# Three attention layers as one sequence of steps, with one list of stages placed between them

## The chip, the cores and the metric

The kernel runs on one core of a Trainium2 chip. The metric is device time in microseconds. The kernel before took 1880.95 us, the median of three runs (1877.2 to 1883.09). Matmuls run on TensorE (PE in the profile), elementwise work on VectorE (DVE), ScalarE (ACT) and GpSimd (POOL), and transfers are issued mostly by SyncE (SP), the indirect ones by POOL.

## The reference

The state x has 4 batches of 512 tokens with 128 features. Four layers follow each other, each of the form: normalize x, run a mixer s and a mixture of experts g on the normalized rows, and add s times silu(g):

```python
xn = _layernorm(x, axis=-1)
s = _L1_attn_ref(xn, ...)           # layer 0: selective scan; 1: causal; 2: rope; 3: distance bias
g = _silu(_L1_ffn_ref(xn, ...))     # experts
x = x + s * g
```

Each attention has 16 heads of 8 features. Layer 1 is causal, and its result is added to xn and normalized again. Layer 2 divides exp(q k) with rope by the sum of exp(q k) without rope, and is normalized again too. Layer 3 subtracts a distance times a slope of the head. The experts are: layer 1, top 2 of 4, with silu(x w1) * (x w3); layer 2, top 2 of 8; layer 3, top 1 of 16, each expert taking at most 160 tokens, those with the highest gate value.

## The kernel before

**Attention.** Work goes by groups: a batch and 4 heads, 16 groups in all. A group takes four steps, one for each block of 128 rows, so an attention has 64 steps, counted k = 0 to 63. In a step, `first_pass` (two heads at a time) makes scores, of which VectorE takes the maximum in layers 1 and 3 (L926) or, in layer 2, the sum of exponentials (L921, L922). `probabilities` makes the scores again transposed and takes the exponential on ScalarE (L956, two per step); in layer 1 POOL clears what lies above the diagonal (`affine_select`, L960). One step later `apply` multiplies with the values (L972). In layers 1 and 3 the first pass runs 8 and 7 steps ahead of the probabilities, so those attentions begin at step -8 and -7; groups are spread (L909) a further four steps ahead.

**Preparing a batch.** `project` (L868 and on) makes q, k and the values of a batch, splits q and k into bf16 parts on ScalarE, VectorE and POOL (L849 to L859, for layer 2 with rope before, L883 to L889), and `spread` moves the parts into the operand blocks by 8 transfers of SP a group (16 in layer 2). After a group `finish` transposes and divides, and after a batch's last group it applies the output matrix.

**Between the instructions of a step** there are two places (`slot`). A place takes jobs due (projects, finishes, the second half of `shift`), then one stage of the list `Work`, and if that was empty, one piece of the generator `beside`, the experts' work of the layer. A piece that ends with "free" uses no engine of the attention, one with "dve" may be followed only in the first place of a step.

**The layers.** Layer 1: its routing (gates, ranks, 32 scatters of rows into expert order, L1232) is `beside` its attention. Its experts (`Routed.run`, L1288 for the first matmuls, L1268 for the second) run behind the attention, 19 tiles of 256 rows. `back` fetches the results of a batch with 8 indirect gathers (L1308), weighs them (L1317, L1318), and `turn` does silu (by exponential and reciprocal, L1333 to L1338), the product and sum (L1340, L1341), the next layer's norm (`rows_norm`, L366 to L382) and the transposes (L1346) of that batch. Batch 0 is turned before attention 2 begins, batches 1 to 3 in its places. Layer 2's experts (`moe2`) are `beside` attention 2. Behind attention 2, `post_norm` (L1104, L1105), `end_layer` (L394 to L400) and `begin_layer` (L319, L326) handle all 16 blocks at once, then attention 3 starts. Layer 3's gate, ranking (L1477 to L1489, 32 pieces), 16 scatters, 16 experts in 18 overlapped rounds (L1555 to L1578) and 16 gathers (L1598) are `moe3`, `beside` attention 3; what is left when the attention ends runs behind it, and `end_layer` closes.

**Order.** Inside `tc.manual_schedule` the listed engines run in the order in which the code is written. For attentions 1 and 2 these are PE, ACT and DVE; SP and POOL are left to the scheduler. For layer 1's experts and attention 3 all five are listed. Each engine runs its queue in order.

Of the kernel before, what the change touches and what calls it, by code (L numbers as in the profile page):

```python
# [2 lines left out]

# [16 lines left out]
P = 128  # L20
# [207 lines left out]
def kernel(ctx: ExitStack, tc: tile.TileContext, ap: dict):  # L228
# [108 lines left out]
    class Work:  # L337


        def __init__(self):  # L340
            self.queue = []

        def add(self, key, stages):
            self.queue.append((key, stages))

        def step(self):

            while self.queue:
                got = next(self.queue[0][1], None)
                if got is not None:  # L350
                    return got
                self.queue.pop(0)

        def need(self, key):

            while any(k == key for k, _ in self.queue):
                self.step()

    work = Work()
# [32 lines left out]
    def end_layer(i, s, y):  # L392
# [3 lines left out]
        out = ap["out"].rearrange("(c p) d -> p c d", p=P) if i == 3 else None  # L396
        for h in range(2):
# [3 lines left out]
            if i == 3:  # L401
                nc.sync.dma_start(out=out[:, cs, :], in_=x[:, cs, :])
# [44 lines left out]
    def weighted_bias(acc, cw, b2, e):  # L447

        for q in range(NC // 4):
# [3 lines left out]
            cwT = small.tile([e, 512], F32, tag="cwT", name="cwT", bufs=1)  # L453
# [68 lines left out]
    def layer0(ctx0, mp, fp, s_out, acc):  # L522
# [182 lines left out]
        with tc.manual_schedule(engines=engines | {mybir.EngineType.SP}):  # L705
# [32 lines left out]
            for n in range(last):  # L738
                now = n
                b, r = divmod(n, 32)  # L740
                if n == 0:
                    in_stages(0, 1)
                    after(2, weighted_bias, acc, cw, b2, E0)
# [40 lines left out]
    def attention(i, lp, xnT, pads, vaug, s_io, beside=iter(()), done=lambda b: None):  # L784
# [9 lines left out]
        wqk = lp.tile([P, 2, P], F32, name="wqk")  # L794
        nc.sync.dma_start(out=wqk, in_=ap[f"a{i}_qk"])
        wvo = lp.tile([P, 2, D], F32, name="wvo")
# [7 lines left out]
        if i == 3:  # L804
            for g in range(NG):
                for m in range(2):
                    nc.sync.dma_start(out=pads["q"][g][m], in_=ap["c_qb"][:, g, m, :])
            qbs = lp.tile([P, 1], F32, name="qbs")
            dve.tensor_scalar(qbs, col("q_b"), QSCALE, None, ALU.mult)
# [20 lines left out]
        def values(b):  # L830
# [5 lines left out]
            if i == 3:  # L836
                vb = lp.tile([P, 4, D], F32, tag="vb", name="vb")
# [6 lines left out]
        def split(t, d, b):  # L844


            tt = pool.tensor_tensor if b else dve.tensor_tensor
            cp = dve.tensor_copy if i == 2 and b else act.copy
# [13 lines left out]
        def project(b):  # L862

            work.need((i - 1, b))
# [4 lines left out]
            t = lp.tile([P, 2, L], F32, tag="qk", name="qk")  # L869
# [10 lines left out]
            if i == 2:  # L880
# [8 lines left out]
                (pool if b else dve).tensor_tensor(r, r, c, ALU.add)  # L889
                parts.append((r, lp.tile([P, 2, PARTS, L], BF16, tag="rparts", name="rparts")))  # L890
                yield 1
            parts.insert(0, (t, lp.tile([P, 2, PARTS, L], BF16, tag="parts", name="parts")))
# [19 lines left out]
        def first_pass(n, qc, m):  # L912
# [10 lines left out]
            else:  # L923
                if qc == 0 and m == 0:
                    s["nm"] = lp.tile([P, 4, 4], F32, tag="nm", name="nm", bufs=2)
                dve.tensor_reduce(s["nm"][:, qc, 2 * m : 2 * m + 2], ps[:, :, :hi], AX.X, ALU.max, negate=True)  # L926

        def shift(n):

            nm = st[n].pop("nm")  # L930
            parts = lp.tile([P, 4, 4, 3], BF16, tag="nmp", name="nmp", bufs=2)
# [8 lines left out]
            rows = lp.tile([12, L], BF16, tag="rows", name="rows", bufs=2)  # L940
# [6 lines left out]
        def probabilities(n, kc, m):  # L947
# [5 lines left out]
            if m == 0:  # L953
                s[kc] = lp.tile([P, 4, L], F32, tag="at", name="at", bufs=3)
# [9 lines left out]
        def apply(n, kc):  # L964
# [11 lines left out]
            if kc == 3:  # L976
                s["osb"] = lp.tile([P, L], F32, tag="osb", name="osb", bufs=2)
                act.copy(s["osb"], s["po"])

        def finish(n):  # L980
# [3 lines left out]
            if g == 0:  # L984
                outs[b] = lp.tile([P, 4, D], F32, tag="o", name="o", bufs=2)
# [5 lines left out]
            rs = lp.tile([P, 4, 4], F32, tag="rs", name="rs", bufs=2)  # L991
# [12 lines left out]
            oT = lp.tile([P, L], F32, tag="oT", name="oT")  # L1004
# [13 lines left out]
        engines = {mybir.EngineType.PE, mybir.EngineType.Activation, mybir.EngineType.DVE}  # L1018
        if i == 3:
            engines |= {mybir.EngineType.Pool, mybir.EngineType.SP}  # L1020


        ahead, lead = {1: (8, 12), 2: (0, 8), 3: (7, 11)}[i]
        jobs = []
        free, went = [None], [False]

        def aside():
            free[0] = next(beside, None)

        def slot(k, second=False):  # L1030

            bank_left = True
            for job in sorted(jobs, key=lambda j: j[0]):
                if job[0] <= k and bank_left:
                    got = next(job[1], None)
                    if got is None:
                        jobs.remove(job)
                    else:  # L1040
                        job[0] = k + 1
                        bank_left = not got
            if bank_left and work.step() is not None:
                return
            was = went[0]
            went[0] = False
            if free[0] == "free" or free[0] == "dve" and not second or free[0] is None and bank_left and (
                i == 2 or not second or not was
            ):
                aside()  # L1050
                went[0] = True

        def begins(k):
# [5 lines left out]
            if r == 0 and n % NG == NG - 1 and n + 1 < last:  # L1059
                jobs.append([k, project(n // NG + 1)])  # L1060

        def step(k):
            begins(k)
            f = k + ahead
            for m in range(2):
                if f < 4 * last:
                    first_pass(f // 4, f % 4, m)
                if m == 1 and k > 0:
                    apply((k - 1) // 4, (k - 1) % 4)
                    if k % 4 == 0:  # L1070
                        jobs.append([k + 1, finish(k // 4 - 1)])
                if k >= 0:
                    probabilities(k // 4, k % 4, m)
                if m == 0:
                    slot(k)
            if i != 2 and f % 4 == 3 and f < 4 * last:
                stages = shift(f // 4)
                next(stages)
                jobs.append([k + 2, stages])
            slot(k, True)  # L1080

        with tc.manual_schedule(engines=engines):
            table[0] = None
# [594 lines left out]
```

## Time and profile before

| what | us |
|---|---|
| median of three runs | 1880.95 |
| the profiled execution's own time | 1882.61 |
| its span, first to last instruction | 1880.9 |
| layer 0 and layer 1's start, to | 540 |
| attention 1, steps -8 to 39 | 540 to 712.8 |
| attention 1, steps 40 to 63 | 712.8 to 782.6 |
| experts of layer 1 | 791.7 to 951.3 |
| from there to attention 2's first exponential | 951.3 to 1015.4 |
| attention 2 | 1015.4 to 1402.2 |
| from there to step -3 of attention 3 | 1402.2 to 1484 |
| attention 3 from step -3 | 1484 to 1826.1 |
| behind it | 1826.1 to 1880.9 |

The bounds of attentions are the exponentials of L956, two a step, and those of the experts the matmuls of L1288 and L1268, as the timeline has them. The profile covers one execution. "Busy" is the time in which an engine works on an instruction; a wait names the engine and line of the instruction that waited and what ended the wait. Busy over the span: PE 72%, DVE 61%, ACT 51%, POOL 27%; the mean clock granted to TensorE is 0.818 of full speed.

### The profile page before, as it was taken

The numbers are of one execution on the slowest core, as the hardware profiler recorded it, in microseconds if no ns is written. First come the engines' busy times: TensorE is split into PE (matmuls) and PEld (weight loads), VectorE is DVE, ScalarE is ACT, GpSimd is POOL, SyncE is SP. The second block draws the span as 40 slices with busy tenths as digits, with TensorE's granted clock in tenths as the row PEclk, the third lists the DMA queues.
The fourth block names the chain that finished last, engine by engine and source line by source line (L and its number), as shares of the span: only waits on it lengthen the run. The fifth ranks groups of instructions, "written<-read, shape, count | busy, mean of one in ns | idle before, by whom it ended". The sixth has DMA issues, their size and how long they took to land.

```text
span 1880.9 us, 22349 instructions
## 1 busy us (share of the span) xinstructions
PE 1361.7 (72%) x7733; PEld 688.8 (37%) x7733; DVE 1145.0 (61%) x1973; ACT 959.4 (51%) x1283; POOL 508.4 (27%) x534
## 2 busy tenths in 40 slices
PE   4778788888567788899933566777872487788870
PEld 2445544545332333388820112233211122233330
DVE  5467678577755667332224777656666799976521
ACT  3565555555325565422215575776982054566550
POOL 1245354444405643211152302102002010041213
PEclk8789888899768888799975767887795588899995
DMA  5558667577224221034223140211300311123102
GB/s 170 142 146 201 165 208 184 142 191 203 63 40 116 47 40 28 1 104 134 82 56 51 28 63 6 41 27 24 50 21 2 79 18 18 18 58 68 49 26 67
DMA packets 119857, 149.48 MB, mean 79 GB/s; under 512 B 15288, under 2 KB 80704, under 8 KB 117952
## 3 DMA queue, kind: packets, MB, share of 16 engines
q1 hardware_dynamic: 112784, 123.40, 28.2%
q0 software_dynamic: 6960, 24.65, 3.9%
q8 instruction: 61, 1.00, 0.2%
q14 instruction: 52, 0.43, 0.1%
HBM read 114.69 MB, written 16.01 MB: 69 GB/s over the span
## 4 chain that ended last, share of the span: by engine, by line
PE 41%; DVE 18%; ACT 15%; issue 11%; DMA 6%; POOL 6%; SPq 2%; POOLq 0%; ACTq 0%; DVEq 0%
PE py L972 6%; PE wide L1288 5%; PE bank L507 5%; PE wide L823 5%; ACT at L956 5%; DMA rep<-ddd 4%; PE py L518 4%; PE py L1268 3%; DVE den L922 2%; DVE nm L926 2%; ACT ep L921 2%; PE wide L827 2%; DVE hs L652 2%; SPq L909 1%; PE wide L868 1%
## 5 line engine op out<-in xcount | busy, mean ns | idle before, releaser
L956 ACT ACTIVATE at<-wide 128x1024 f32<-128x1024 f32 (+3 forms) x384 | 356.9, 936 | 226.5 <-PE wide L827 118.6
L926 DVE TENSOR_REDUCE nm<-wide 128x2 f32<-128x1024 f32 (+3 forms) x256 | 256.1, 1018 | 92.0 <-PE wide L827 91.5
L972 PE MATMUL py<-at,vaug 128*32 128x512 f32 (+3 forms) x1536 | 240.7, 653 | 23.8 <-POOL at L960 17.9
L823 PE MATMUL wide<-k,q 48*128 48x512 bf16 (+4 forms) x768 | 167.9, 415 | 105.9 <-DMA k<-parts 47.9
L922 DVE TENSOR_REDUCE den<-ep 128x2 f32<-128x1024 f32 x128 | 155.4, 1216 | 126.2 <-ACT ep L921 125.3
L654 POOL TENSOR_TENSOR hc<-hs,C 128x512 f32<-128x512 f32 x128 | 163.1, 1279 | 252.8 <-DVE hs L652 142.5
L507 PE MATMUL bank<-xnT,w 128*128 128x512 f32 x256 | 151.6, 748 | 75.5 <-ACT h L508 57.9
L921 ACT ACTIVATE ep<-wide 128x1024 f32<-128x1024 f32 x128 | 137.8, 1077 | 58.1 <-PE wide L823 47.5
L652 DVE TENSOR_TENSOR_SCAN hs<-dA,dBx 128x512 f32<-128x512 f32 x128 | 154.7, 1209 | 0.6 <-POOL hc L654 0.6
L518 PE MATMUL py<-w,h 128*128 128x128 f32 x1024 | 128.7, 287 | 19.0 <-DVE acc L468 19.0
L518 PEld LDWEIGHTS py<-w,h 128*128 128x128 f32 x1024 | 126.5, 203 | 38.1 <-DVE acc L468 27.4
L641 ACT ACTIVATE dA<-rep,A 128x512 f32<-128x512 f32 x128 | 87.3, 715 | 99.4 <-DVE hs L652 66.8
L648 DVE TENSOR_TENSOR dBx<-B,rep 128x512 f32<-128x512 f32 x128 | 89.0, 696 | 55.9 <-DMA rep<-ddd 38.1
L823 PEld LDWEIGHTS <-q 48*128 48x128 bf16 (+1 forms) x768 | 50.7, 97 | 197.0 <-issue 142.7
L507 PEld LDWEIGHTS bank<-xnT,w 128*128 128x128 f32 x256 | 58.8, 240 | 168.0 <-ACT h L508 77.6
L827 PE MATMUL wide<-own_bf 128*128 128x128 bf16 x768 | 119.1, 242 | 0.0
L823 PE MATMUL wide<-q,k 63*128 63x512 bf16 (+3 forms) x512 | 96.4, 376 | 24.1 <-ACT at L956 13.1
L1288 PE MATMUL wide<-xT,w 128*128 128x256 f32 x456 | 109.1, 390 | 1.5 <-ACT h L1291 0.8
L508 ACT ACTIVATE h<-bank,cols 128x512 f32<-128x512 f32 x128 | 84.7, 687 | 44.9 <-PE bank L507 44.4
L1292 DVE TENSOR_TENSOR h<-h,wide 128x512 f32<-128x512 f32 x57 | 39.2, 688 | 108.2 <-ACT h L1291 108.2
L823 PE MATMUL wide<-qr,kr 48*128 48x512 bf16 x256 | 62.8, 461 | 44.7 <-ACT ep L921 39.6
L1288 PEld LDWEIGHTS wide<-xT,w 128*128 128x128 f32 x456 | 84.3, 195 | 15.7 <-issue 3.7
(334 smaller groups left out, 2024.4 us busy)
## 6 DMA issues: line engine op xcount, KB each, us to landing
rep<-ddd SPq DMA_DIRECT2D x256, 256.0 KB
q<-parts SPq DMA_DIRECT2D x192, 48.0 KB
k<-parts SPq DMA_DIRECT2D x192, 48.0 KB
w<-in_f_w_dram SPq DMA_DIRECT2D x18, 256.0 KB
ddd<-dd POOLq DMA_DIRECT2D x8, 512.0 KB, 3.0
w<-in_f_w_dram SPq DMA_DIRECT2D x32, 128.0 KB
qr<-rparts SPq DMA_DIRECT2D x64, 48.0 KB
kr<-rparts SPq DMA_DIRECT2D x64, 48.0 KB
```

Source lines behind the costliest of these rows:

```text
L507: pe.matmul(ph, w1[:, f * P : (f + 1) * P], self.xnT[:, tb * L : (tb + 1) * L], start=True, stop=True)
L518: pe.matmul(py[:, cs], h[:, f, cs], w2[:, f, :], start=(f == 0), stop=(f == 3))
L652: dve.tensor_tensor_scan(h, st[n]["dA"], st[n]["dBx"], 0.0, ALU.mult, ALU.add)
L654: pool.tensor_tensor(hc, h, batch[tiles[n][0]]["C"], ALU.mult)
L823: pe.matmul(ps[:, j, lo:hi], lhs[m][r, cs], rhs[m][r, lo:hi], start=True, stop=not own)
L827: pe.matmul(ps[:, j, cs], ident_bf, mask_bf if causal else diag_bf[:, h + j, :], start=False, stop=True)
L921: act.activation(e, ps, AF.Exp)
L922: dve.tensor_reduce(s["den"][:, qc, 2 * m : 2 * m + 2], e, AX.X, ALU.add)
L926: dve.tensor_reduce(s["nm"][:, qc, 2 * m : 2 * m + 2], ps[:, :, :hi], AX.X, ALU.max, negate=True)
L956: act.activation(a[:, :, lo:], ps[:, :, lo:], AF.Exp)
L972: pe.matmul(s["po"][32 * j : 32 * j + 32, lo:], vaug[b % 2][:, kc, 4 * g + j, :], a[:, j, lo:], start=kc == 0, stop=kc == 3,)
L1288: pe.matmul(ph[:, g, m * SLOT1 : (m + 1) * SLOT1], wk[:, f + g, m, :], self.x[k], start=True, stop=True)
```

## The change

The three attentions become objects with `first` (the project of batch 0), `begins`, `step` and `behind`, and the main program walks through their steps. One object, `Places`, holds jobs, stages and the generators beside for all of them. A place now takes up to two stages of the list; a piece beside that ends with "dve" may also be followed in the second place of every third step.

- All five engines are in written order from attention 1 to the end.
- Layer 1's experts run after step 39 of attention 1 (`PAUSE = 40`). Behind them come steps 40 to 63, in whose places batches 0 to 2 are fetched, weighed and turned; batch 3 follows in attention 2. The two gathers of a block stand in one stage, two stages to a block.
- The first project of attention 2 is a stage list in attention 1's places (from step 51), and its first spreads follow in steps 56 to 63.
- Layer 2's output is normalized and turned by batch, when both its attention and its experts have finished the batch (`both`).
- The first project of attention 3 stands in steps 53 to 55 of attention 2, its spreads and its steps -7 to -4 beside steps 56 to 63. The distance rows of its operand blocks are written in steps 8 to 14 of attention 2, by 16 small transfers.
- `moe3` begins when no batch of layer 2 is left to be turned, which in written order is step 3 of attention 3. Its ranking then stands in steps 8 to 31 (before: -5 to 27), and four of its 18 expert rounds stand behind step 63 (before: none).
- Layer 3 ends by batch (`end_layer3`).
- `split` takes POOL for its subtractions except in layer 1's batch 0, and VectorE for all casts of layer 2. The column of ones in the values stays in layer 2. Some tiles share buffers.

```diff
-        with tc.tile_pool(name="route1", bufs=1) as rp:
...
-                    attention(1, lp, xnT, pads, vaug, s, routed.route(), lambda b: work.add((0, b), post_rows(1, s, b)))
...
-                    routed.run(fp)
-                    xnT = keep.tile([P, N], F32, name="xnT")
-                    for b in range(B):
-                        work.add((1, b), routed.back(b, acc, xnT))
-                    work.need((1, 0))
...
-                attention(2, lp, xnT, pads, vaug, s, moe2(fp, xnT, acc))
-        post_norm(2, s)
-        end_layer(2, s, acc)
-        xnT = begin_layer(s)
...
-            attention(3, lp, xnT, pads, vaug, s, moe3(rp, s, xnT, acc))
-        end_layer(3, s, acc)
+                for k in range(-8, PAUSE):
+                    a1.step(k)
+                a1.behind(PAUSE)
+                while places.beside:
+                    places.aside()
+                with tc.tile_pool(name="moe1", bufs=1) as fp:
+                    routed.run(fp)
...
+            for b in range(2):
+                places.add(("fetch", b), routed.fetch(b, acc))
+            for b in range(2):
+                turn1(b)
+            for k in range(PAUSE, a1.steps):
+                a1.step(k)
+                if k == a1.steps - 14:
+                    places.add("first2", a2.first, after=(1, 0))
+                if k >= a1.steps - 8:
+                    places.need("first2")
+                    a2.begins(k - a1.steps)
...
+            for k in range(a2.steps):
+                a2.step(k)
+                if k in range(8, 16, 2):
+                    a3.distances((k - 8) // 2)
+                if k == a2.steps - 12:
+                    places.add("first3", a3.first, after=(2, 0))
+                if k >= a2.steps - 8:
+                    places.need("first3")
+                    k3 = k - a2.steps - 3
+                    if k3 < -7:
+                        a3.begins(k3)
+                    else:
+                        a3.step(k3, False)
...
+                places.beside.append(moe3(rp, s, xnT, acc, done3))
+                for k in range(-3, a3.steps):
+                    a3.step(k)
```

The place, and the fetch of a batch:

```diff
+        def place(self, second=False):
+            bank_left = True
...
+            for n in range(2):
+                got = self.work() if bank_left else None
+                if got is None:
+                    break
+                bank_left = not got
+                if n:
+                    return
+            was, self.went = self.went, False
+            dve_left = not second or self.now % 3 == 0
+            if self.needs == "free" or self.needs == "dve" and dve_left or self.needs is None and bank_left and (
+                self.every or not second or not was
+            ):
+                self.aside()
+                self.went = True
...
+        def fetch(self, b, y):
+
+            yg = self.got[b] = self.room()
             for c in range(4):
+                self.gather(y[:, 4 * b + c, :], 0, 4 * b + c)
+                self.gather(yg[:, c, :], 1, 4 * b + c)
+                for _ in range(2):
+                    yield 0
```

## The prediction

> **What bounds the kernel now.** I read the page's slices first, then busy time by stage, then the waits inside the two stages in which TensorE is nearly idle, then the groups of instructions.
>
> ```profile
> PE   4778788888567788899933566777872487788870
> PEclk8789888899768888799975767887795588899995
> ```
>
> A slice is 47 us. TensorE falls to 3 behind the experts of layer 1 (slices 20, 21) and to 2 and 4 between attentions 2 and 3 (slices 30, 31). I cut the span there: a stage ends with the last exponential of L956 of an attention, or the last matmul of an expert.
>
> ```profile
> core 0: us, PE busy (x) PEld busy (x) DVE busy (x) ACT busy (x) POOL busy (x), PEclk, DMA share, GB/s
> 712.80:782.60 69.80, 59.59 (x466) 21.44 (x467) 37.16 (x84) 40.38 (x62) 22.21 (x50) 0.86 0.11 16
> 791.70:951.30 159.60, 158.25 (x948) 141.32 (x948) 49.04 (x93) 43.72 (x79) 17.23 (x17) 0.98 0.30 95
> 951.30:1015.40 64.10, 10.23 (x27) 4.27 (x26) 16.02 (x36) 15.71 (x22) 30.79 (x29) 0.58 0.24 55
> 1015.40:1402.20 386.80, 274.37 (x1412) 94.69 (x1410) 258.37 (x377) 281.12 (x320) 53.45 (x34) 0.77 0.22 35
> 1402.20:1484.00 81.80, 27.06 (x129) 14.01 (x125) 50.68 (x133) 13.88 (x21) 10.15 (x9) 0.60 0.17 44
> 1540.00:1661.80 121.80, 99.44 (x650) 35.02 (x649) 110.84 (x177) 61.74 (x69) 10.39 (x9) 0.87 0.16 26
> 1826.10:1880.90 54.80, 9.85 (x40) 5.69 (x40) 9.33 (x12) 4.80 (x4) 16.13 (x16) 0.55 0.22 62
> ```
>
> Experts: TensorE alone (158 of 160). Attention 2 (1015 to 1402): no engine full. Steps 8 to 31 of attention 3 (from 1540): VectorE, 111 of 122. In the two gaps, 64 and 82 us, no engine is full; they are chains:
>
> ```profile
> PE wide L823 <- DMA k<-parts: 27.2, 1, 27.2
> PE bank L1346 <- DVE s L382: 21.2, 1, 21.2
> ...
> PE bank L326 <- DVE s L319: 25.6, 1, 25.6
> PE wide L823 <- DMA k<-parts: 10.9, 1, 10.9
> ```
>
> The first two lie in the first gap (gathers, silu, norm, then split and spread of q and k), the last two in the second.
>
> **What the change removes.** (a) Layer 1's experts come behind step 39, not 63. The 9.1 us from the last exponential (782.6) to the first expert matmul go; about 2 remain for the last product, and two jobs of step 40 move into the experts, some 2 us of TensorE. The first 16 expert matmuls took 6.54 us cold, later ones 3.54: 3 us less. Net **-7**. (b) In the first gap the steps 40 to 63 now stand, which themselves only move; 64.1 shrinks to two seams of 2 us: **-60**. (c) The second gap goes: attention 3's steps -7 to -4 stand beside attention 2's last four, its first project before them; step -3 began at 1484. 81.8 becomes a seam of 2: **-80**. (d) Table loads at L372 and L373, 8 of 1.28 us, mostly go; ScalarE waits for TensorE in attention 1: **-2**. Sum **-149**, if what filled the gaps were free elsewhere. It is not.
>
> **Attention 1, steps 40 to 63: +50.** Before, these 24 steps took 69.8 us with nothing placed. POOL runs in order, and each step's second affine select, which the next step's product of probabilities and values needs, now stands behind gathers.
>
> ```profile
> L960 POOL TENSOR_SCALAR_AFFINE_SELECT at<-at 128x256 f32<-128x256 f32 x128 | 52.9, 421 | 89.8 <-ACT at L956 89.3
> L1308 POOL DMA_INDIRECT yg<-ys,pos x16 | 16.4, 1026 | 4.8 <-issue 4.6 <-POOL acc L1338 0.3
> L1232 POOL DMA_INDIRECT xs<-acc,pos x32 | 31.8, 994 | 65.8 <-DVE pos L1205 40.4 <-DMA xs<-acc,pos 21.5 <-issue 4.0
> L1336 DVE RECIPROCAL yg<-yg 128x512 f32<-128x512 f32 x3 | 10.1, 3353 | 0.1
> ```
>
> Steps 40 to 43 place four gathers each: 4 x 1.3 (1.03 and 0.3 issue) + 2 x 0.42 = 6.1 us a step, 24 for four that took 11.9; with 2 for the last ys write (POOL waits for it): +14 (between 0, if three buffers of probabilities absorb it, and 16). Steps 52 to 56 place layer 2's first rope and splits on POOL (2 x 2.4, 2 x 2.3, 4 x 1.25 = 14.4) and eight gathers (10.4), with selects 29 us, unevenly, for five steps that took 16: +16. The turn of a batch costs VectorE 13 us (8 weighing ops 3.4, reciprocal 3.35, the one before it 0.7, two products 1.4, norm 4.3). Two stand in steps 44 to 50, whose maxima and jobs are 18: 42 for steps that took 18.5, part of it falling where POOL holds everybody up, so +16. The third stands in steps 58 to 60, where no maxima are left: +4, the transposes waiting for the norm. In these steps up to two placed stages go at once, so POOL's product waits on the reciprocal with selects behind it.
>
> Here a rule speaks against the change. The Trainium skill, "SBUF — State Buffer", section "A bandwidth-pool intuition that's wrong (but worth ruling out)": a DMA whose descriptors GpSimd writes takes 620 ns alone and 3100 ns beside a VectorE copy. The 32 scatters of L1232 ran in attention 1 beside VectorE's work and took 994 ns each, the gathers 1026 with VectorE nearly idle. By the rule 24 gathers among selects would cost 24 x 2.5 = 60 us more; by the row nothing. I take the row and keep part of the 60 for the high end.
>
> **Attention 2: +17.** Before, three turns stood in steps 0 to 18, which took 115 us where undisturbed steps (48 on) take 3.7: 48 us over, of which I count 39 as theirs, their VectorE time. Now there is one in steps 6 to 10, with its post norm (+5 on VectorE), and three of layer 2 at 14.6 (no weighing, with post norm), in steps 19 to 24, 35 to 40 and 51 to 56. I charge 16, 12, 12 and 6 (the last has slack, 2 x 1.22 of 3.7 busy): 46, so +7. Bounds: 0 each to 21.2 each, the longest wait for a turn's transposes. Attention 3's first project (matmuls 3.6, values 1.2): +5. Its four steps add 2 x 1.14 of maxima to VectorE's 2.44 and two pairs of matmuls: 4.9 against 3.7, +5. Layer 2's experts have the same pieces as before, some ten steps earlier. Subtractions of batch 0 go from VectorE (1.22) to POOL (2.28), which is idle there; batch 0 of layer 2 takes its casts from ScalarE to VectorE, some 7 us, hidden while the selects hold steps 52 to 56, otherwise up to 7 more. SP, like POOL, is now in written order: a group of attention 2 issues 16 transfers of 0.7 in four steps (11 of 15 us), and attention 3's 16 distance transfers fall into steps 8 to 14 (another 11): 34 of some 40 us, hidden; they replace eight that stood in the second gap.
>
> **Attention 3: +15.** The ranking (32 pieces of about 2.2 us of VectorE) cannot start before layer 2's last batch is turned: it moves from steps -5 to 27 into steps 8 to 31, at four pieces in three steps. Steps 8 to 31 had 20 pieces in 121.8 us; 12 more are 26 us where VectorE is 91% busy: +23. Steps -3 to 7 lose 12 pieces (26) and take the last turn, post norm and gate (19), with a wait for the transposes: -4. In steps 32 to 63 fourteen expert rounds stand where eighteen did; steps with a round took 5.7 (45 to 62), those before 4.7 (32 to 44): four times 1.0, -4.
>
> **Tail: +4.** Four expert rounds now run after the last step, uncovered: 2.7 each (matmuls 0.8 and 0.8, the two biases 0.7, some latency; between 1.6, TensorE alone, and 6, one after the other): +11. The end is by batch:
>
> ```profile
> 1867.75 1.28 ACT L394 ACT_TABLE_LOAD   x1 [38.85 <-DMA acc<-obuf,slot]
> 1869.04 1.91 ACT L394 ACTIVATE acc<-acc 128x2048 f32<-128x2048 f32 x1
> 1870.99 2.36 DVE L399 TENSOR_TENSOR s<-s,acc 128x1024 f32<-128x1024 f32 x2 [28.80 <-ACT acc L394]
> ```
>
> Table load and three batches go ahead during the gathers; after the last, silu 0.6, two products of 0.7 and a smaller store remain where 13 us stood: -7.
>
> **Sum.** -149 + 50 + 17 + 15 + 4 = **-63**. The profiled execution took 1882.61 us (span 1880.9, 1.7 around it) and becomes 1819.6. It lies 1.7 above the median of the three runs, 1880.95; the same -63 from there gives **1818**.
>
> **Rivals.** (1) *The placed work is hidden*: gathers absorbed, turns in slack: +20, +5, +5 and 0 for the four stages: **1762**. For it: no engine is over 73% in attention 2. Against: steps 0 to 18 lost 48 us to three turns and little else. (2) *It is dearer*: turns at 14 instead of 9.5 each, POOL's descriptors partly starved: some +35, **1853**. For it: the waits above. (3) *Slower*: TensorE's queue is in order, and each of the eight turns ends in transposes waiting for VectorE's norm. I charge the eight 76 in all (20 in attention 1, 46 in attention 2, 10 in attention 3). If each costs the 21.2 us of the longest such wait, they cost 170, 94 more: **1912**. It decides from (76 + 63) / 8 = 17.4 each. Against: three turns cost 48 together at most. (4) *The change doesn't do what it says*: POOL holds back the first splits of the next attention so long that TensorE waits for the spreads at its step 0, and the gaps reappear beside the placed cost. The four waits shown above are 85 us; if three quarters come back the gain is gone: **1882**. Group 0 has eight steps (18 us before) for 16 DMA issues of 0.7 and 2.75 to land, 14: narrow, but a few us late is only a few us.
>
> **How the numbers follow.** My sum 0.50, hidden 0.22, dearer 0.20, slower 0.06, no effect 0.02. A measurement tells 0.3% (5.6 us) from no change; faster 0.92, same 0.02, slower 0.06. Low 1762 is the hidden case, high 1860 the dearer one with its own spread; the likeliest one's own range is 1790 to 1842.
>
> **What would show it.** Right: no stretch over 5 us without TensorE between the experts and attention 2, or between attentions 2 and 3; steps 40 to 63 near 120 us, attention 2 near 404, steps -3 to 63 of attention 3 near 357, the tail near 59; POOL named as releaser of the products in steps 40 to 43 and 52 to 56. Wrong: these steps near 70 to 90 (hidden), a wait of TensorE for VectorE over 17 us at each turn's transposes (slower), or the k and q spreads named at step 0 of attention 2.

## The result and the profile after

The changed kernel takes 1887.15 us, the median of 18 runs (1878.53 to 1896.68), beside 1879.1 for the kernel before (18 runs, 1869.74 to 1888.7). The ratio is 1.0041, 95% interval 1.0023 to 1.0059: 0.4% slower. I had predicted 1818, in a range from 1762 to 1860. Below, 0.1% is 1.9 us, and every ratio is to the kernel before in the same set of runs.

The profiled execution took 1891.87 us, with a span of 1890.1. First the slices of the page of the kernel after, to be held against those of before:

```profile
PE   4778788888668889997644568485757777789862
PEclk9789888899758789998676757688778687689995
```

The 2 and 4 between attentions 2 and 3 (slices 30 and 31) are now 7 and 7, the 3 and 3 of slices 20 and 21 are 4 and 4. But slice 25, in the middle of attention 2, has gone from 7 to 4, and 27 and 29 from 7 to 5. The stages say how much each is worth. The columns are the stretch, its length, busy time of PE, PEld, DVE, ACT and POOL (with counts), the granted clock, the DMA share and GB/s. An attention's bounds are now the exponentials of L1007, which was L956. The first line begins 3 us behind the first expert matmul, which started at 709.4; the experts took 162.8 us in all.

```profile
712.50:872.20 159.70, 157.47 (x965) 140.32 (x964) 46.55 (x79) 42.97 (x79) 15.82 (x16) 0.99 0.32 100
872.20:1006.60 134.40, 77.99 (x473) 26.57 (x474) 82.50 (x181) 43.15 (x74) 64.76 (x84) 0.70 0.19 40
1006.60:1009.40 2.80, 2.04 (x16) 0.98 (x14) 0.00 (x0) 1.81 (x4) 0.41 (x1) 0.85 0.01 3
1009.40:1451.80 442.40, 283.71 (x1466) 102.50 (x1464) 292.09 (x442) 287.37 (x339) 69.18 (x46) 0.75 0.20 31
1451.80:1524.40 72.60, 58.45 (x313) 25.48 (x311) 52.79 (x97) 29.06 (x42) 9.14 (x9) 0.72 0.19 56
1524.40:1672.60 148.20, 113.97 (x648) 36.33 (x647) 133.47 (x215) 61.85 (x69) 4.49 (x3) 0.76 0.13 20
1672.60:1830.70 158.10, 134.33 (x926) 55.71 (x927) 89.79 (x147) 98.46 (x144) 40.07 (x47) 0.95 0.21 53
1830.70:1890.10 59.40, 17.33 (x68) 10.80 (x64) 13.85 (x24) 8.84 (x16) 19.06 (x20) 0.59 0.22 62
```

| stage | after, us | my sum | missed by |
|---|---|---|---|
| experts of layer 1, from 709.4 | 162.8 | 160 to 162 | +1 |
| attention 1, steps 40 to 63 | 134.4 | 120 | +14 |
| seam to attention 2 | 2.8 | 2 | +1 |
| attention 2 | 442.4 | 404 | +38 |
| from its end to attention 3's step 8 | 72.6 | 54 | +19 |
| attention 3, steps 8 to 31 | 148.2 | 145 | +3 |
| attention 3, steps 32 to 63 | 158.1 | 160 | -2 |
| tail | 59.4 | 59 | 0 |

(54 is 56 for steps -3 to 7 before, less the 4 of my sum, and a seam of 2.) The gaps closed as I had said. The miss of some 72 us, that of the profiled execution, lies in three stages. Each stage time here and below comes from one execution. Attention 3's steps 8 to 31 took 148.2 us here and between 140 and 150 in the profiles of the other kernels that place the same ranking there, so a difference of 5 us in one stage says little. The waits of the kernel after show what is new there (engine, what it waited for, total, times, longest; the first two and the last line are of the whole span, the others of attention 2):

```profile
PE bank L1365 <- DVE s L429: 64.0, 7, 16.3
PE py L1023 <- POOL at L1011: 23.2, 14, 8.5
...
PE wide L873 <- ACT ep L972: 61.6, 32, 17.3
DVE part L1386 <- DMA left<-in_f_b_dram: 18.2, 1, 18.2
ACT r_r L419 <- DVE r_ve L416: 48.2, 8, 13.2
...
ACT r_r L419 <- DVE r_ve L416: 82.1, 14, 13.2
```

In the kernel before, ScalarE's wait for VectorE's variance (at the logarithm of the norm, then L372) was this in attention 2, to be held against the 48.2:

```profile
ACT r_r L372 <- DVE r_ve L369: 10.8, 3, 4.0
```

One turn, that of layer 2's batch 0 in steps 23 and 24 of attention 2 (20.0 and 14.0 us), shows how they hang together. This is the timeline of the kernel after, engine by engine (start, length, engine, line, operation, and in brackets the idle time before it and what ended it):

```profile
1190.05 3.35 DVE L1355 RECIPROCAL room<-room 128x512 f32<-128x512 f32 x1
...
1195.88 2.60 DVE L1359 TENSOR_TENSOR s<-s,acc 128x512 f32<-128x512 f32 x1
1198.52 2.49 DVE L1360 TENSOR_TENSOR x<-x,s 128x512 f32<-128x512 f32 x1
...
1202.77 0.17 DVE L416 TENSOR_SCALAR r_ve<-r_mv 128x4 f32<-128x4 f32 x1
...
1206.28 1.11 DVE L429 TENSOR_SCALAR s<-x,r_mv,r_r 128x128 f32<-128x128 f32 x4
...
1202.97 0.21 ACT L419 ACTIVATE r_r<-r_ve 128x4 f32<-128x4 f32 x1 [12.47 <-DVE r_ve L416]
...
1206.68 1.24 PE L1365 MATMUL bank<-cst,s 128*128 128x128 f32 x4 [16.25 <-DVE s L429]
...
1195.51 2.43 POOL L901 TENSOR_TENSOR qk<-qk,parts 128x1024 f32<-128x1024 f32 x1 [0.69 <-DVE parts L900]
1197.90 2.56 POOL L901 TENSOR_TENSOR qkr<-qkr,rparts 128x1024 f32<-128x1024 f32 x1
```

Reciprocal, product, norm and transposes were placed within three places, so little attention work stands between them in any queue. While VectorE walks through its part, ScalarE's logarithm and TensorE's transposes are at the head of their queues, and exponentials and scores of later steps stand behind them: ScalarE is idle 12.5 us, TensorE 16.25. VectorE then waits 1.4 and 2.2 us for exponentials that came late.

My theory after this look: what was missed is mostly **order**, dependent stages two to a place. The rivals: **volume**, that VectorE's amount of work sets attention 2 and any order gives the same; **one late load** (the 18.2 us of L1386); and **POOL beside VectorE** (the products of L1359 and L1360 took 2.5 us, where others took 0.7).

### The profile page after: what moved, and what is told of

Read it like the earlier page. It is cut to its first block, busy times and chain, and to the rows that moved or that the text cites. A ratio compares the mean times of both kernels' runs of the same rounds, so it can differ in the third digit from the quotient of the medians.

```text
span 1890.1 us, 22415 instructions
## 1 busy us (share of the span) xinstructions
PE 1386.0 (73%) x7733; PEld 697.1 (37%) x7733; DVE 1183.5 (63%) x2019; ACT 946.3 (50%) x1286; POOL 526.9 (28%) x545
## 4 chain that ended last, share of the span: by engine, by line
PE 44%; ACT 17%; DVE 16%; issue 10%; DMA 7%; POOL 4%; SPq 2%; ACTq 0%; POOLq 0%; DVEq 0%
PE py L1023 7%; PE wide L873 7%; ACT at L1007 6%; PE bank L559 5%; PE wide L1304 5%; DMA rep<-ddd 4%; PE py L570 3%; PE wide L877 3%; ACT ep L972 2%; PE py L1284 2%; DVE den L973 2%; DVE hs L704 2%; DVE nm L977 2%; ACT dA L693 1%; PE wide L919 1%
## 5 line engine op out<-in xcount | busy, mean ns | idle before, releaser
L1007 ACT ACTIVATE at<-wide 128x1024 f32<-128x1024 f32 (+3 forms) x384 | 356.1, 933 | 253.5 <-PE wide L877 128.4
L1023 PE MATMUL py<-at,vaug 128*32 128x512 f32 (+3 forms) x1536 | 252.5, 687 | 32.0 <-POOL at L1011 23.2
L973 DVE TENSOR_REDUCE den<-ep 128x2 f32<-128x1024 f32 x128 | 155.6, 1216 | 117.6 <-ACT ep L972 111.3
L570 PE MATMUL py<-w,h 128*128 128x128 f32 x1024 | 128.4, 287 | 18.8 <-DVE acc L520 18.8
L559 PEld LDWEIGHTS bank<-xnT,w 128*128 128x128 f32 x256 | 58.8, 240 | 170.8 <-ACT h L560 77.0
L873 PE MATMUL wide<-q,k 63*128 63x512 bf16 (+3 forms) x512 | 101.8, 397 | 23.0 <-ACT at L1007 16.8
```

Of the source, the lines that this page charges most:

```text
L559: pe.matmul(ph, w1[:, f * P : (f + 1) * P], self.xnT[:, tb * L : (tb + 1) * L], start=True, stop=True)
L570: pe.matmul(py[:, cs], h[:, f, cs], w2[:, f, :], start=(f == 0), stop=(f == 3))
L873: pe.matmul(ps[:, j, lo:hi], lhs[m][r, cs], rhs[m][r, lo:hi], start=True, stop=not own)
L973: dve.tensor_reduce(s["den"][:, qc, 2 * m : 2 * m + 2], e, AX.X, ALU.add)
L1007: act.activation(a[:, :, lo:], ps[:, :, lo:], AF.Exp)
L1023: pe.matmul(s["po"][32 * j : 32 * j + 32, lo:], vaug[b % 2][:, kc, 4 * g + j, :], a[:, j, lo:], start=kc == 0, stop=kc == 3,)
```

## The experiments

### Dependent stages apart

One dependent stage is put to a place: behind each, `"wait"` ends the list's share of that place, and the logarithm has a stage of its own.

```diff
-                if got is None:
+                if got is None or got == "wait":
                     break
...
+    def apart(b):
+        if b < B - 1:
+            yield "wait"
...
         dve.tensor_scalar(ve, mv[:, :, 1], EPS, None, ALU.add)
         r = small.tile([P, 4], F32, tag="r_r", name="r_r")
+        if b < B - 1:
+            yield 0
+            yield "wait"
         use_exp()
         act.activation(r, ve, AF.Ln)
         act.activation(r, r, AF.Exp, scale=-0.5)
         yield 0
+        yield from apart(b)
```

`turn` has `yield from apart(b)` behind each of its stages too. This is the form of the second run below, in which batch 3 keeps the old order; the first run had it for all batches.

> The stages of a turn and of a norm that depend on each other stand one to a place instead of two, and the logarithm has a stage of its own; all work stays. The kernel after takes 1887 us, and in it TensorE waits 64.0 us for the normed rows at the turns' transposes, ScalarE 81 us for their statistics. Order theory (what these turns cost is queues standing behind dependent stages): 30 to 50 us less, near 1845, and both waits at half or less. Volume theory (VectorE's amount of work in attention 2 sets it, 292 of 442 us): within 8 us of 1887, the waits only move to other lines.

1841.43 us, ratio 0.9787 (0.9742 to 0.9833). But in this order layer 3's gate stood ahead of the last turn, so it read batch 3's rows before they were turned, and its ranking began in step 6 of attention 3 where it begins in step 8 of the kernel after. The second form leaves the gate where it was:

> The stages of turns and norms one to a place, as in the first run, for batches 0 to 2; batch 3 of each layer keeps two to a place, so the order of attention 3 is that of the kernel after (in the first run layer 3's gate had moved ahead of the last turn, which moved its ranking forward too and gave it rows not yet turned). Order theory: the gain of the first run stands, 35 to 50 us less than after, 1837 to 1852, in attention 1's steps 40 to 63 (134 to about 115 us) and attention 2 (442 to about 418). If the first run's gain came from the gate moved forward: within 10 us of 1887.

1850.61 us, 0.9843 (0.9809 to 0.9877): 37 us less than after (1.0041 - 0.9843), with every instruction kept. These are attention 1's steps 40 to 63 and attention 2, and then the two waits over the whole span:

```profile
873.80:988.00 114.20, 75.67 (x468) 25.12 (x469) 69.84 (x152) 41.03 (x69) 62.28 (x82) 0.72 0.23 47
991.10:1408.70 417.60, 291.34 (x1471) 103.87 (x1469) 291.81 (x471) 288.47 (x343) 69.05 (x47) 0.74 0.21 33
PE bank L1378 <- DVE s L437: 12.5, 5, 6.8
ACT r_r L426 <- DVE r_ve L420: 30.8, 8, 9.0
```

The two stages fall from 134.4 to 114.2 us and from 442.4 to 417.6; TensorE's wait for the normed rows falls from 64.0 to 12.5, ScalarE's for the variance from 82.1 to 30.8. The granted clock is not the reason: it was 0.70 and 0.75 in these stages of after, and 0.72 and 0.74 here. Order is the largest part of the miss. Where it helped is less clear than the two stage times suggest. Spread out, the turn of layer 1's batch 2 no longer fits into attention 1: its reciprocal runs in step 59 of attention 1 in after, and in step 2 of attention 2 here. So the first stage holds one turn fewer (12.7 us less VectorE work), and attention 2 is 25 us shorter with one turn more. The turns' products also no longer run beside a POOL subtraction (below).

### Taking the waits away, not the work

> Leaves out the turned rows: the transposes of all eight turns read the identity matrix, so TensorE waits there for nothing of VectorE; every instruction stays. TensorE waited 64.0 us at these transposes. My recorded rival (3), TensorE's in-order queue behind the norm: 40 to 60 us less, near 1837. If VectorE or ScalarE is what is late and TensorE only the last to show it: at most 10 us less, and the wait turns up at the next product or exponential.

```diff
-            pe.transpose(pt[:, c * P : (c + 1) * P], sb[:, c, :], ident)
+            pe.transpose(pt[:, c * P : (c + 1) * P], ident, ident)
```

1864.61 us, 0.9911 (0.9880 to 0.9942), 24 us less than after, between the two expectations (40 to 60, or at most 10). ScalarE still waited 78.8 us for the variance (82.1 in after).

> As the run before it, and the logarithm of the norm's variance is replaced by an exponential of zeros, so ScalarE does not wait for the statistics either (left out: the turned rows and the norm's scale). ScalarE waited 81 us at the logarithm, 48 of it in attention 2. If the two waits are links of one chain: 10 to 30 us below the run without TensorE's wait, near 1815, which is my prediction. If VectorE's volume sets it: no more than 5 us below it.

```diff
-        act.activation(r, ve, AF.Ln)
+        act.activation(r, zero[:, :4], AF.Exp)
```

1843.04 us, 0.9815 (0.9778 to 0.9853), 42 us less than after. So TensorE's wait, the one that my rival (3) named, is worth about 24 us where it shows 64, and ScalarE's at the logarithm another 18 where it shows 82: the queues stand at the same time, and part of each wait is covered. Both together give about what the better order gives. Two limits: the rows that the next layer reads are no longer the turned ones in these runs, so its routing changes too; and in the first of them some 18 us of the gain lie in the two attentions, the rest in attention 3, whose steps 8 to 31 ran at a granted clock of 0.84 there and 0.76 in after.

### The late load

In the kernel after SP issues layer 2's expert loads in written order, one place ahead of their first use.

> Only the loads of layer 2's experts are issued earlier (from step 50 of attention 1, six pieces ahead of their first use). In the kernel after VectorE waits 18.2 us once for the last bias load, in step 2 of attention 2, which takes 21.5 us. If that wait lies on the path: 15 to 20 us less, near 1870. If the queues behind it catch up in the next steps: 0 to 5 us less.

```diff
                 if k == a1.steps - 14:
+                    places.beside.append(moe2(fp, xnT, acc, done2))
                     places.add("first2", a2.first, after=(1, 0))
...
-            places.beside.append(moe2(fp, xnT, acc, done2))
```

In `moe2`, six `yield "free"` follow the loads. 1876.28 us, 0.9981 (0.9967 to 0.9995): 11 us less than after, between the two expectations. The wait is gone; by the difference, about 7 of its 18 us had been made up in later steps. Both together:

> As the run before it, and layer 2's expert loads issued early. If the two costs are separate, they add: 11 us below that run, near 1832, with attention 2 near 405, which is what I had predicted for it (404). If the stalls hide each other: within 4 us of it.

1839.59 us, 0.9793 (0.9757 to 0.9828), and in a second set of runs:

> The kernel with stages apart and loads early once more, beside the run after it, in more rounds: near 1839.6 (0.979 of before).

1831.47 us, 0.9761 (0.9722 to 0.9800). The costs add, and this kernel is faster than before and after. Its stages, from steps 40 to 63 of attention 1 to attention 3's step 8, and then the tail:

```profile
867.70:982.10 114.40, 73.44 (x468) 25.10 (x470) 72.44 (x162) 41.23 (x69) 62.40 (x82) 0.76 0.24 52
985.20:1391.50 406.30, 287.56 (x1471) 103.13 (x1469) 288.95 (x461) 288.53 (x343) 68.84 (x47) 0.76 0.21 33
1391.50:1464.10 72.60, 57.76 (x316) 25.52 (x314) 54.21 (x99) 29.43 (x42) 9.15 (x9) 0.74 0.18 56
...
1770.30:1829.70 59.40, 17.32 (x68) 10.78 (x65) 13.86 (x24) 8.86 (x16) 19.03 (x20) 0.59 0.22 62
```

Attention 2 at 406 is where I had predicted it (404), the steps 40 to 63 lie 6 under. That is partly luck: my sum had three turns in the one and four in the other, and this kernel has two and five. Attention 3's start has not moved: 72.6, as in after.

### Each half of the change undone

> Undoes one half of the change: layer 2 is normalized and turned behind attention 2, and attention 3 starts then, as in the kernel before; the rest is as after. By the terms that I had predicted this half is worth 21 us (80 saved, 59 paid), so the run would be near 1908. If the turns cost what steps 23, 24, 39, 40 and 51 to 56 of attention 2 show in the kernel after (some 64 us over 3.7 a step), this half is a loss, and the run is faster than after, near 1856.

```diff
-                if k == a2.steps - 12:
-                    places.add("first3", a3.first, after=(2, 0))
...
-                        a3.step(k3, False)
             a2.behind(a2.steps)
...
+            for h in range(2):
+                turns = [turn(b, s, acc, room, xnT) for b in (2 * h, 2 * h + 1)]
...
+            for _ in a3.first:
+                pass
...
-                for k in range(-3, a3.steps):
+                for k in range(-7, a3.steps):
```

1892.05 us, 1.0071 (1.0034 to 1.0107): 6 us slower than after, a difference that the two overlapping intervals do not settle; not 21 slower and not 30 faster, so neither expectation held. And with the stages apart and the loads early:

> Layer 2 turned behind attention 2 again, with the stages apart and the loads early. Undoing this half cost the kernel after only 5 us, where I had priced it at 21. If the blocked queues took the difference: 20 to 35 us more than 1839.6, near 1865. If not: within 10 us of it.

1851.43 us, 0.9855 (0.9819 to 0.9891), 12 to 18 us above the two runs of the kernel with this half, less than the 20 to 35 that I had expected if the blocked queues took the difference. Its stages, attention 2, the gap up to step 0 of attention 3, attention 3, tail:

```profile
984.50:1344.10 359.60, 268.76 (x1423) 96.55 (x1421) 244.97 (x337) 275.03 (x316) 56.91 (x38) 0.80 0.21 34
1344.10:1461.10 117.00, 36.24 (x155) 18.98 (x151) 76.88 (x193) 17.96 (x40) 17.41 (x15) 0.56 0.16 41
1461.10:1805.50 344.40, 281.58 (x1822) 108.47 (x1824) 254.29 (x400) 187.74 (x249) 52.13 (x57) 0.86 0.17 37
1805.50:1847.20 41.70, 6.49 (x28) 3.53 (x28) 8.16 (x13) 5.41 (x7) 16.17 (x16) 0.57 0.22 62
```

Here the account of this half can be read off. The gap of 117.0 shrinks to 16.8 (1391.5 to step 0 at 1408.3): 100 saved. Attention 2 grows from 359.6 to 406.3, 46.7; attention 3 from 344.4 to 362.0, 17.6; the tail from 41.7 to 59.4, 17.7: 82 paid, 18 left. In attention 2 VectorE gets 44.0 us more work (244.97 to 288.95) and the stage gets 46.7 longer, although VectorE is busy only 68% of it before and 71% after. TensorE gets 18.8 us more and ScalarE 13.5, so the length alone does not name VectorE. The chain of work that ended last does: followed back through this stretch, it lies on VectorE for 142 us where it lay there for 87, and on the other two engines together for 200 where it was 214. With blocked queues, in the kernel after, the same moved work made the stage 58.8 longer (383.6 in the undone kernel, 442.4).

A caveat: this gap is not that of the kernel before, which had 93.0 us from attention 2's last exponential to step 0 (1402.2 to 1495.2). My undone gap turns two batches at a time in written order. Against a gap of 93 this half would lose 6 us (18 - 24); that is an estimate from these stages and was not run.

> Undoes the other half: layer 1's experts run behind the whole of attention 1, batch 0 is turned before attention 2 and batches 1 to 3 in it. By the terms that I had predicted this half saves 69, pays 50 in attention 1 and takes 23 out of attention 2: the run would be 42 us slower than after, near 1929. If this half gives nothing either: within 10 us of 1887.

```diff
-        PAUSE = 40
+        PAUSE = 64
...
-            for b in range(2):
+            for b in range(B):
                 places.add(("fetch", b), routed.fetch(b, acc))
-            for b in range(2):
                 turn1(b)
...
+            places.need((1, 0))
+            for _ in a2.first:
+                pass
```

1877.13 us, 0.9985 (0.9970 to 1.0001): 11 us *faster* than after. This half, which I had priced at a gain of 42, was a loss. Steps 40 to 63, then experts and gap, then attention 2 of this kernel:

```profile
706.10:775.10 69.00, 57.93 (x467) 21.33 (x468) 37.02 (x83) 40.45 (x62) 21.54 (x49) 0.88 0.13 21
775.10:1001.90 226.80, 169.17 (x1001) 146.27 (x1001) 77.42 (x142) 51.88 (x93) 52.44 (x45) 0.88 0.28 84
1001.90:1440.20 438.30, 289.77 (x1459) 103.87 (x1459) 300.79 (x477) 290.57 (x344) 77.12 (x54) 0.74 0.21 35
```

69.0 + 226.8 = 295.8 us up to attention 2; the kernel after needs 159.7 + 134.4 + 2.8 = 296.9. The gap of 67 us (226.8 less 159.7) had gone, and the steps 40 to 63 gave all of it back, 134.4 for 69.0. Attention 2 takes 438.3 here with three turns of layer 1 and no late load; after has one, and 442.4.

> Layer 1's experts behind the whole of attention 1 again, now with the stages apart and the loads early. Undoing this half took 10 us off the kernel after, where I had priced it at 42 more. If the half was spoilt by the blocked queues: 20 to 40 us more than 1839.6, near 1870. If it is no gain in itself: within 10 us of 1839.6, or less.

1863.08 us, 0.9900 (0.9865 to 0.9934), 20 to 26 us more than the two runs with this half. With the stages apart the half is a gain. Up to attention 2 this kernel takes 294.6 us (706.7 to 1001.3), the one with the half 279.8 (705.4 to 985.2); attention 2 takes 426.7 and 406.3. Some 11 us of this are not the half's: spread out, the turn of batch 1 was not done when its project was due, and had to be finished at once in step 4, which took 16.3 us where the kernel with the half took 5.1.

### The last turn, in attention 3's start

> Leaves out the norm and the turn of layer 2's last batch (attention 3 reads that batch's old rows), the only turn that stands in attention 3's start. That start took 18 us more than I had priced, 10 us of it for this turn. If the turn is the whole of the miss: 25 us or more less than 1839.6, near 1813. If it costs what I charged: near 1830, and the 18 us lie elsewhere in steps -3 to 7.

```diff
-                places.add((2, b), post_rows(2, s, b))
-                places.add((2, b), turn(b, s, acc, room, xnT))
+                if b < B - 1:
+                    places.add((2, b), post_rows(2, s, b))
+                    places.add((2, b), turn(b, s, acc, room, xnT))
```

1819.86 us, 0.9682 (0.9653 to 0.9710), 15 to 21 us less than the two runs of the same kernel with the turn. The edit does more than it says, though. With no turn to wait for, layer 3's gate moved ahead of step 0 of attention 3 (it stood in step 3), the ranking began in step 6 and not 8, and the tail fell from 59.4 to 49.8 us. So the run shows the turn and a gate moved forward together. The stretch from attention 2's end to step 8 fell from 72.6 to 59.6:

```profile
1391.60:1451.20 59.60, 52.74 (x307) 24.18 (x306) 43.99 (x64) 27.32 (x36) 5.00 (x4) 0.77 0.23 68
```

The total lies between the two expectations, but it cannot be split between the turn and the gate. What the trace shows is where the time of this stretch goes. In the kernel after, step 3 of attention 3 took 14.8 us (3.6 in the kernel before), and in it stands the gate: 32 matmuls in one block, behind which VectorE waits for scores. Before, the same block stood in the gap between the attentions, and took half as long. TensorE and VectorE of after, then TensorE of before:

```profile
1494.92 6.95 PE L460 MATMUL bank<-gates,xnT 128*128 128x16 f32 x32
1502.78 1.23 DVE L977 TENSOR_REDUCE nm<-wide 128x2 f32<-128x1024 f32 x1 [9.12 <-PE wide L877]
```

```profile
1445.15 3.74 PE L408 MATMUL bank<-gates,xnT 128*128 128x16 f32 x32 [0.78 <-DVE vb L838]
```

The granted clock was 0.51 in the 20.4 us of after around the block (from 1486.2), and 0.97 in the 6.8 us around it before (from 1443.0). In the run without TensorE's wait the block took 3.74 us again, and step 3 took 7.4. No run moved the gate alone.

### POOL beside VectorE

> The best run so far (stages apart, loads early; 1839.6 us) with layer 2's subtractions on VectorE instead of POOL. In the traces VectorE's products of 128x512 take 0.7 us alone and 2.5 beside a POOL subtraction, its casts 0.68 and 1.8. If this slowing lies on the path: 5 to 15 us less, though VectorE gets 4 times 4.9 us more to do. If VectorE's volume counts: 10 to 20 us more, near 1855.

```diff
-            alone = i == 1 and b == 0
+            alone = i == 2 or i == 1 and b == 0
```

1832.62 us, 0.9761 (0.9716 to 0.9805): within the interval of the kernel that it was made from. So the edit was run on the kernel after alone, and again beside its original:

> The kernel after with one edit: layer 2's subtractions on VectorE instead of POOL. If the slowing of VectorE beside POOL is a part of the 70 us that I missed: 7 to 15 us less than 1887. If the 20 us of added VectorE work and the shorter operations cancel: within 5 us of it.

> The same with the subtractions on VectorE, measured before at 1832.6 (0.976), within the interval of the other. If the slowing beside POOL counts on the path: 5 to 10 us below the run before it. If not: within 3 us of it.

On the kernel after: 1876.16 us, 0.9990 (0.9970 to 1.0011), 10 us less. On the spaced kernel: 1833.03 us, 0.9751 (0.9722 to 0.9781), the same as its original in the same set (0.9761). One reason is that little of the slowing is left there. With the subtractions still on POOL, the products of the spaced kernel take their short time in every turn, because the spacing moved them off the subtractions; only casts still stand beside one:

```profile
L1370 DVE TENSOR_TENSOR s<-s,acc 128x512 f32<-128x512 f32 x8 | 5.7, 716 | 2.7 <-POOL acc L1367 2.7
L911 DVE CAST rparts<-qkr 128x1024 bf16<-128x1024 f32 x4 | 6.6, 1640 | 0.0
```

Whether what is left is also covered, as the other queues no longer stand behind VectorE, these runs don't tell. And some of the 37 us that I put down to order are the products' short time.

## Why the prediction was wrong

- **Removed, -149: right.** No expert gap was left, and the seams took 2.8 us and 5.6 (the 16.8 to step 0 less the 11.2 that steps -3 to -1 took before). The tail and steps 8 to 63 of attention 3 are within 3 us of my sum.
- **The tail's +4: right in sum, wrong in both terms, which is luck.** Against the kernel with layer 2 turned behind attention 2 (41.7), ending by batch gains 13 and not 7 (54.8 to 41.7), and the uncovered expert rounds cost 18 and not 11.
- **Attention 1, +50: measured +65.** The step that failed is "two turns cost 16 and the third 4": I charged VectorE's time, part of it hidden, and put the standing of the other queues at next to nothing. The starts of the exponentials in the two traces split the stage by steps:

  | steps of attention 1 | before, us | after, us | more | charged |
  |---|---|---|---|---|
  | 40 to 43, gathers | 11.9 | 18.9 | 7 | 14 |
  | 44 to 50, two turns | 18.7 | 45.6 | 27 | 16 |
  | 52 to 56, first project and gathers | 16.2 | 29.7 | 14 | 16 |
  | 58 to 60, third turn | 6.3 | 20.9 | 15 | 4 |

  The turns' steps cost 42 where I charged 20; POOL's part cost 9 less than I charged, which hid some of it. TensorE's waits in this stage say the same: 25.8 us for the normed rows, 17.5 for POOL's select. I had taken the gathers from their row and not from the starved descriptors of the Trainium skill's "SBUF — State Buffer" (in the section that the prediction names); with the 60 us of that rule the stretch would have been +110. The 32 gathers of after took 1.01 us each, the longest 1.11, so the row was the better guide. I had seen that "up to two placed stages go at once" and charged only POOL's product for it.
- **Attention 2, +17: measured +56.** Three terms failed. *The late load* was missing from my sum: I followed SP's spreads and distance rows past its queue, and not `moe2`'s own loads, which had been early only because SP was scheduled freely before; a wait of 18 us, worth 11. *The turns* were charged 16, 12, 12 and 6 as though VectorE's idle third were slack; the order cost at least 25 more (442.4 to 417.6, with one turn more), and even without that the stage grew by about the VectorE work that was added. *The credit of 23* for two turns moved out of attention 2 was too high: with them there and no late load it took 438.3; with the one turn that is left and the loads early (the run with that edit alone) it took 428.3, so they are worth 10.
- **Attention 3, +15: measured +35 with its start.** "-4 for steps -3 to 7" failed: the stretch took 72.6 for my 54. Some 4 of the 19 us lie before step 0, 11 in step 3, where the gate stands. I had charged the gate in VectorE's time alone (in the 19 for "last turn, post norm and gate") and put its 7 us of TensorE, at half the clock that it had in the gap, at nothing. That is read from the trace and was not tested by a run of its own.
- **The rival that came true in sign, (3),** named one in-order queue. TensorE did wait at seven turns, 9.1 us each and not 21.2, and those waits were worth 24 us. It was ScalarE's logarithm as well, in a queue that I had not looked at because its wait in attention 2 was 10.8 us before.

In all: order 37 us, late load 11, POOL's slowing up to 10 where the queues are blocked (not on top of the first). Order and load bring 1887 to between 1831 and 1840, 13 to 22 us from my 1818. In that kernel's stages only one is still more than 6 us from my sum, attention 3's start (72.6 for 54).

## What to carry to other kernels

Work placed into the gaps of an in-order program costs by how its dependent stages are spaced: leave enough of the host's work between two links of a chain in *every* queue that the chain passes, and let the chain take longer instead. An engine that is busy two thirds of a stage has no slack by that alone: here 44 us more on VectorE came with a stage 47 us longer. Charge a piece of work on every engine that it uses, not only on the busiest. And when an engine goes from free scheduling to written order, follow every one of its loads to its first use, not only the new ones.

## What the runs showed of the hardware

Some of VectorE's operations took two to four times as long beside a POOL subtraction. These are groups of the kernel after, and then of the one with layer 2's subtractions on VectorE (total, mean ns of one):

```profile
L1359 DVE TENSOR_TENSOR s<-s,acc 128x512 f32<-128x512 f32 x8 | 9.7, 1209 | 4.7 <-POOL acc L1357 4.7
L1360 DVE TENSOR_TENSOR x<-x,s 128x512 f32<-128x512 f32 x8 | 9.2, 1152 | 0.3
L903 DVE CAST rparts<-qkr 128x1024 bf16<-128x1024 f32 x4 | 6.5, 1637 | 0.0
```

```profile
L1359 DVE TENSOR_TENSOR s<-s,acc 128x512 f32<-128x512 f32 x8 | 5.8, 729 | 2.5 <-POOL acc L1357 2.5
L1360 DVE TENSOR_TENSOR x<-x,s 128x512 f32<-128x512 f32 x8 | 5.6, 702 | 0.3
L903 DVE CAST rparts<-qkr 128x1024 bf16<-128x1024 f32 x4 | 2.7, 685 | 0.0
```

In after the mean of L1359 is made of six of 0.75 us and two of 2.60, the two beside POOL. The reduction of 128x1024 at L973 was not slowed: 1.22 us alone, 1.20 beside POOL, on average. The Trainium skill's "SBUF — State Buffer", section "Who interferes with whom", says that a VectorE instruction with two SBUF inputs, or in a two-port mode, and a GpSimd instruction that reads SBUF block each other, so that the one issued second stands until the first is done, and that one with a single input outside those modes does not. The rows of the products and of the reduction agree; that the cast ran in such a mode no run here shows. I had weighed the same page for the gathers alone, and not for the subtractions that the change gave to POOL beside the turns.
